# A further product in the Silu slot, statistics one piece per chunk, and gate projections in their inputs' banks: a fused attention-and-Mamba kernel

## The chip, the cores and the metric

The kernel runs on one core of one Trainium2 chip, as one launch. The metric is the device time of that core in microseconds, as the median of several executions. The engines are called PE (TensorE), DVE (VectorE), ACT (ScalarE), POOL (GpSimd) and SP (SyncE, which here issues every DMA).

## The reference, cut to what matters

`x` has 8 samples of 512 channels and 48 x 48 = 2304 tokens, in float32. Layer 0 is a linear causal attention with 8 heads on a group-normalised input, layer 1 a chain of four Mamba blocks over 128 channels each, on another group norm; each block takes the block before it as an addend.

```python
def reference(x, ...):
    x = x + _L0_conv_ref(_gn(x), Wq, bq, Wkv, bkv)      # linear causal attention
    x = x + _L1_conv_ref(_gn(x), in_proj_w, conv_w, ...)  # four Mamba blocks in a chain
    return x

def _mamba(u, Wi, wc, bc, Wx, Wdt, bdt, A_log, Dp, Wo):
    xz = u @ Wi.T
    xp, z = split(xz)                       # 256 inner channels each
    xs = silu(causal_conv4(xp, wc) + bc)
    dt, Bm, Cm = split(xs @ Wx.T)           # 8, 16 and 16 columns
    delta = softplus(dt @ Wdt.T + bdt)
    dA = exp(delta * A)                     # per channel d and state n
    dBu = (delta * xs) * Bm
    h_t = dA_t * h_{t-1} + dBu_t            # scan over 2304 tokens
    y = sum_n(h * Cm) + xs * Dp
    return (y * silu(z)) @ Wo.T

# around each block i: x_i = spx[i] + prev
fused = max(x_i, x_m)
prev = sigmoid(mean(x_i)) * x_i + sigmoid(mean(fused)) * fused
```

## The kernel before

**Jobs, slots and halves.** Tokens are cut in six chunks of 384. A *job* is one chunk of one Mamba block of one sample, 192 in all. Two streams of samples (even and odd) alternate by a fixed list of turns, since the blocks of one sample depend on each other. A job has eight *slots*; in each slot DVE does four scans (`scan`, L830) of 128 partitions x 385, each with its own pair of state and channel group. A slot has two *halves*: half 2k lies before the scans of slot k, and half 2k+1 after its second scan. At each half `beside(half)` steps other tasks that are due, so everything that isn't a scan is dealt out by half numbers. A job's halves run from 0 to 15 modulo 16; slot 7 holds 14 and 15.

**What a scan needs.** Its decays, `exp(delta * A)`, are made by ACT into a PSUM bank (`decay`, L819). Its input is a product of B and `delta * xs` in a tile `u`: the last 128 columns by POOL (`last_product`, L798), the first 256 by DVE (`product`, L809), which reads a PSUM copy `dxp` that ACT makes twice a job (`inputs`, L782). After the scans of a slot POOL multiplies u by C (`weigh`, L846) and PE gathers the sum into `yp` (`gather`, L853). There are five u buffers. In `slot(k)` the product of slot k+1 is drawn at the start of slot k, and the POOL part of slot k+2 in the middle of it.

**Banks.** Six PSUM banks serve everything but `yp` and `dxp`. `ahead(n)` makes decays in advance, up to n, while a bank is spare: DEPTH = 3 after each scan, DEPTH + 2 ahead of the table changes. `take` hands out the bank that has been spare longest, and prefers for decays those that were freed "late".

**A job's inputs.** `prepare` is a task that begins 22 halves (LEAD = 11 slots) before its job's first half, `first = 2 * self.start`, as far as its stream has declared the input `ready`. It convolves two halves of the channels on PE (`conv`, L635: eight records each), makes two gate projections (`gate`, L646), then four Silus on ACT (L670 to L675), then a projection to dt, B and C (L681, L686), then softplus (L694, L705). The Silus and softplus each need another ACT table than the exponential, so each is fenced by table loads. A stage is written `yield when, banks`; "1" means one half after the last stage, "2" two.

```python
yield "1", 1
xc0 = conv(0)
yield "2", 2
xc1 = conv(1)
zp0 = gate(0)
yield "1", 0
```

**Attention.** `chunk(m)` is one chunk of attention for 128 channels, one per job, with its stages at `times[m] + j`. `times[m]` is 3 modulo 16 in the steady part. Among its stages are the projections (L288), the features (L300, L301; L345 for q, L353 for k), the transposition of the divisor (L418) and, after the last chunk of a block, the group norm for Mamba (`group_norm`, L171 to L195), whose result lets `Stream.pass_on` make the next block's input (`xi`, L597 to L609).

**Input statistics.** `statistics(b)` loads 24 pieces of a sample (`piece`, L248) and takes `bn_stats` of each (L242), one piece every two halves, from 64 halves before the sample's attention begins. One buffer `stats_a` serves all samples.

Of the kernel before, what the change touches and what calls it, by code (L numbers as in the profile page):

```python
# [9 lines left out]
F32 = mybir.dt.float32  # L10
AF = mybir.ActivationFunctionType
# [38 lines left out]
def attention_then_mamba_kernel(  # L50
# [110 lines left out]

    def group_norm(stats, n, name, bufs):


        bank = Banks()
        yield "1", 1
        mv = small.tile([P, n, 2], F32, tag=f"mv{n}", name=f"mv_{name}", bufs=1)
# [3 lines left out]
        nc.tensor.matmul(mean_ps[:, 0:n], grp, mv[:, :, 0], start=True, stop=True)  # L171
        yield "1", 0
        gm = small.tile([P, 3, n], F32, tag=f"gm{n}", name=f"gm_{name}", bufs=1)
# [7 lines left out]
        else:  # L181
            nc.vector.tensor_mul(gm[:, 2, :], gm[:, 1, :], gm[:, 1, :])
            nc.vector.tensor_add(gm[:, 2, :], gm[:, 2, :], mv[:, :, 1])
        yield "0", 1
        var_ps = bank()
        nc.tensor.matmul(var_ps[:, 0:n], grp, gm[:, 2, :], start=True, stop=True)
        yield "1", 0
        nc.vector.tensor_scalar_add(gm[:, 2, :], var_ps[:, 0:n], 1e-5)
        bank.free()
        norm = small.tile([P, 3, n], F32, tag=f"norm{n}", name=f"norm_{name}", bufs=bufs)  # L190
        nc.gpsimd.tensor_tensor(norm[:, 0, :], gm[:, 2, :], power[:, 0:n], ALU.pow)
        yield "1", 0
        for i, factor in ((0, -1.0), (1, float(L))):
# [15 lines left out]
    def statistics(b):  # L209

        xv = x[b].rearrange("(t p) l -> p t l", p=P)
        stats = small.tile([P, 4, NC, 6], F32, tag="stats_a", name=f"stats_a{b}", bufs=1)
        if b == 0:

            xs = []

            def load(c):
                t = mpool.tile([P, 4, 1 + LC], F32, tag="u", name=f"xs_{c}", bufs=5)[:, :, 0:LC]
                nc.sync.dma_start(out=t, in_=xv[:, :, c * LC : (c + 1) * LC])
                xs.append(t)  # L220

            for c in range(5):
                load(c)
            load_projections(0)
            for c in range(NC):
                for ct in range(4):
                    nc.vector.bn_stats(stats[:, ct, c, :], xs[c][:, ct, :])
                if c == 0:
                    load(5)
                    fetch(0)  # L230
            for o in range(1, 4):
                load_projections(o)
        else:
            for ct in range(4):
                for c in range(NC):
                    yield "2", 0
                    if (ct, c) == (0, 0):
                        nxt = piece(b, 0)
                    xs = nxt
                    i = ct * NC + c + 1  # L240
                    nxt = piece(b, i) if i < 4 * NC else None
                    nc.vector.bn_stats(stats[:, ct, c, :], xs)  # L242
        norms[b] = yield from group_norm(stats, 4, f"a{b}", 2)
# [24 lines left out]
    def chunk(m):  # L268
# [99 lines left out]
        if ksum is not None:  # L368
            kept = new("kept")
            nc.scalar.copy(kept[64:128], kc[64:128])  # L370
            save(ksum[:, cols], kept[64:128])
# [84 lines left out]
        if c + 1 == NC:  # L456
            norm = yield from group_norm(stats, 1, f"m{b}_{o}", 8)
            flush()
            done[b, o] = norm
# [156 lines left out]
    class Job:  # L616
# [6 lines left out]
        def prepare(self):  # L623
# [19 lines left out]

            def gate(h):
                zp = bank()[:, 0:LC]
                nc.tensor.matmul(  # L646
# [5 lines left out]
                )  # L652
                return zp

# [3 lines left out]
            converting.append(n)  # L658
            yield "1", 1
            xc0 = conv(0)  # L660
            yield "2", 2
            xc1 = conv(1)
            zp0 = gate(0)
            yield "1", 0
            xs = self.xs = mpool.tile([P, 2, LC], F32, tag="xs", name=f"xs_{n}")
# [4 lines left out]
            nc.scalar.activation(xs[:, 0, :], xc0, AF.Silu, bias=pv[:, 0:1])  # L670
            bank.free()
            zp1 = gate(1)
            nc.scalar.activation(xs[:, 1, :], xc1, AF.Silu, bias=pv[:, 1:2])
            nc.scalar.activation(sz[0], zp0, AF.Silu)
            nc.scalar.activation(sz[1], zp1, AF.Silu)  # L675
            converting.clear()
            bank.free(3, late=True)
            yield "1", 1
# [65 lines left out]
            for h in range(2):  # L744
                yield "1", 0
                nc.gpsimd.tensor_tensor(delta[:, h, :], delta[:, h, :], xs[:, h, :], ALU.mult)  # L746
            first = 2 * self.start
            yield "2", 0
# [208 lines left out]
    def finale(job):  # L957
# [4 lines left out]
        if job.c == NC - 1:  # L962
            yield from job.stream.pass_on()

    begun, put, counted = 0, 0, list(range(1, B))

    def begin(latest):

        nonlocal begun, put
        while counted and times[parts.index((counted[0], 0, 0))] - 64 <= half_no[0]:  # L970
            tasks.append(Task(statistics(counted.pop(0))))
# [60 lines left out]
    todo = 0  # L1032
    primed = set()

# [32 lines left out]
    def slot(k):  # L1067
        job, s = at(k)
        end = k + 1 == slots or apart(k + 1)
        if not end:  # L1070
            j, r = at(k + 1)
            j.product(r, us[k + 1])
# [7 lines left out]
        for i in range(4):  # L1080
# [4 lines left out]
            if i == 1:  # L1085
# [10 lines left out]
                if not end and k + 2 < slots and not apart(k + 2):  # L1096
                    j, r = at(k + 2)
                    us[k + 2] = j.last_product(r)
                beside(2 * k + 1)
        u = us[k]  # L1100
# [91 lines left out]
```

## Time and profile before

| what | value |
|---|---|
| median of 3 runs | 9328.11 us |
| lowest and highest | 9324.06 and 9329.19 us |
| profiled execution, time | 9323.3 us |
| profiled execution, span | 9321.5 us |
| mean granted TensorE clock | 0.948 |
| instructions | 120629 |
| DMA, mean | 176 GB/s, 1642.84 MB |

In a group's row stand the line, the engine, the operation, the tiles out<-in, the shapes and the count; then the total busy time in us and the mean of one in ns; then the idle time of the engine ahead of it and what ended most of it. In a row of the timeline stand start and length in us, and in square brackets the idle time before it and its releaser. A matmul in float32 shows as two records.

| row | count | mean of one |
|---|---|---|
| scan, L830 | 6144 | 938 ns |
| decay, L819 | 6144 | 579 ns |
| product, L809 | 1536 | 1195 ns |
| POOL's part of the product, L798 | 1536 | 1276 ns |
| product with C, L846 | 1536 | 3180 ns |
| bn_stats of the input, L242 | 168 | 542 ns |
| table load ahead of the Silus, L670 | 192 | 1283 ns |
| table load ahead of softplus, L705 | 192 | 1283 ns |
| table loads ahead of decays, L819 | 382 | 1283 ns |
| gate projection records, L646 | 768 | 500 ns |

The busy times of neighbouring instructions overlap a little: scans follow each other at 0.85 us, pieces of bn_stats at 0.46.

### The profile page before, as it was taken

How to read it: one execution, taken by the hardware profiler on the slowest of the kernel's cores; microseconds unless marked ns; L12 is line 12 of the kernel's file. 1: busy time of each engine (PE TensorE's matmuls, PEld its weight loads, DVE VectorE, ACT ScalarE, POOL GpSimd, SP SyncE). 2: the span in 40 equal slices, each digit the busy share in tenths (PEclk: the TensorE clock that was granted, in tenths of full speed). 3: DMA queues.
4: the chain of work that ended last, by engine and by line, in shares of the span. 5: the costliest groups of instructions: out<-in, count | busy, mean ns of one | idle time of the engine just before them, and what ended most of it. 6: DMA issues, size and time to landing. Idle time of an engine off the chain costs nothing.

```text
span 9321.5 us, 120629 instructions
## 1 busy us (share of the span) xinstructions
PE 7735.1 (83%) x35714; PEld 3673.0 (39%) x35714; DVE 8348.4 (90%) x11640; ACT 6580.2 (71%) x12656; POOL 8080.8 (87%) x5635
## 2 busy tenths in 40 slices
PE   7888888888888888888888888888888888888865
PEld 4444444433344444443343444443333434444321
DVE  3899999999999999999999999999999999999997
ACT  3677777777777777777777777776777777777775
POOL 2788888889988898889998888888998888888998
PEclk9999999999999999999999999999999999999977
DMA  6566666667666666666766666667666666666654
GB/s 189 158 169 173 175 174 168 180 189 198 188 169 176 177 179 172 176 183 189 196 182 178 174 175 173 174 170 194 192 184 182 176 176 172 173 171 175 167 153 129
DMA packets 1002899, 1642.84 MB, mean 176 GB/s; under 512 B 138592, under 2 KB 797312, under 8 KB 1002240
## 3 DMA queue, kind: packets, MB, share of 16 engines
q1 hardware_dynamic: 1002240, 1635.13, 64.1%
q8 instruction: 283, 4.64, 0.2%
q14 instruction: 376, 3.08, 0.1%
HBM read 1309.06 MB, written 325.58 MB: 175 GB/s over the span
## 4 chain that ended last, share of the span: by engine, by line
DVE 39%; ACT 20%; PE 18%; issue 7%; DMA 7%; POOL 6%; SPq 2%; DVEq 0%; POOLq 0%; ACTq 0%
DVE u L830 23%; DVE u L809 8%; PE bank L288 7%; ACT bank L819 6%; PE bank L635 4%; POOL u L846 4%; ACT L819 3%; PE yp L853 3%; PE bank L646 2%; ACT L705 2%; DMA B<-scr 2%; DMA C<-scr 1%; ACT bank L301 1%; ACT delta L705 1%; DVE sm L436 1%
## 5 line engine op out<-in xcount | busy, mean ns | idle before, releaser
L830 DVE TENSOR_TENSOR_SCAN u<-bank,u 128x385 f32<-128x385 f32 (+1 forms) x6144 | 5475.1, 938 | 530.5 <-ACT bank L819 503.2
L846 POOL TENSOR_TENSOR u<-u,C 128x1536 f32<-128x1536 f32 x1536 | 4885.1, 3180 | 219.5 <-DVE u L830 112.6
L819 ACT ACTIVATE bank<-dr,av 128x385 f32<-128x385 f32 (+1 forms) x6144 | 3431.3, 579 | 1556.9 <-DVE u L830 1113.3
L853 PE MATMUL yp<-u,cst 128*64 128x384 f32 x12288 | 2429.9, 514 | 282.7 <-ACT yp L787 146.3
L798 POOL TENSOR_TENSOR u<-B,dxr 128x512 f32<-128x512 f32 x1536 | 1959.9, 1276 | 22.4 <-DMA dxr<-xscr 19.0
L288 PE MATMUL bank<-xn,wq_sb 128*128 128x384 f32 x4608 | 1855.1, 552 | 48.8 <-DVE u L830 31.7
L809 DVE TENSOR_TENSOR u<-B,dxp 128x1024 f32<-128x1024 f32 x1536 | 1834.7, 1195 | 10.7 <-ACT dxp L782 10.7
L853 PEld LDWEIGHTS yp<-u,cst 128*64 128x64 f32 x12288 | 788.3, 139 | 1476.6 <-issue 903.5
L635 PE MATMUL bank<-xi,wk 128*128 128x384 f32 x3072 | 1118.2, 507 | 280.1 <-ACT kl L385 172.7
L288 PEld LDWEIGHTS bank<-xn,wq_sb 128*128 128x128 f32 x4608 | 929.1, 212 | 862.9 <-issue 215.1
L635 PEld LDWEIGHTS bank<-xi,wk 128*128 128x128 f32 x3072 | 563.7, 193 | 862.2 <-ACT kl L385 254.1
L844 POOL COPY state<-u 128x4 f32<-128x4 f32 x1280 | 243.8, 190 | 740.6 <-DVE u L830 738.0
L300 ACT ACTIVATE ex<-bank,bqkv_sb 128x384 f32<-128x384 f32 x384 | 221.3, 576 | 561.6 <-PE bank L288 539.2
L787 ACT ACTIVATE yp<-xs,pv 128x384 f32<-128x384 f32 x384 | 223.4, 582 | 405.7 <-DVE yz L865 405.7
L819 ACT ACT_TABLE_LOAD x382 | 490.1, 1283 | 6.7
L746 POOL TENSOR_TENSOR delta<-delta,xs 128x384 f32<-128x384 f32 x384 | 385.8, 1005 | 95.5 <-DMA dscr<-delta 84.3
L418 PE MATMUL bank<-cst,rdb 128*128 128x128 f32 x576 | 112.7, 310 | 426.1 <-DVE u L830 334.7
L694 PE MATMUL bank<-dbc,wd 9*128 9x384 f32 x768 | 316.3, 524 | 65.1 <-ACT dbc L686 29.0
L646 PE MATMUL bank<-xi,wi 128*128 128x384 f32 x768 | 297.8, 500 | 59.8 <-ACT xs L670 59.8
L871 PE MATMUL bank<-yz,wo 128*128 128x384 f32 x768 | 297.6, 509 | 34.1 <-DVE yz L865 19.4
L449 PE MATMUL bank<-sm,v 128*64 128x128 f32 x2304 | 257.2, 301 | 42.4 <-DVE u L830 40.6
L418 PEld LDWEIGHTS bank<-cst,rdb 128*128 128x128 f32 x576 | 66.8, 153 | 558.9 <-ACT xb L601 272.5
(109 smaller groups left out, 7860.3 us busy)
## 6 DMA issues: line engine op xcount, KB each, us to landing
B<-scr SPq DMA_DIRECT2D x1536, 192.0 KB
C<-scr SPq DMA_DIRECT2D x1536, 192.0 KB
xn<-xn SPq DMA_DIRECT2D x192, 768.0 KB
dr<-dscr SPq DMA_DIRECT2D x768, 192.0 KB
dxr<-xscr SPq DMA_DIRECT2D x768, 192.0 KB
dscr<-delta SPq DMA_DIRECT2D x192, 384.0 KB
xscr<-delta SPq DMA_DIRECT2D x192, 384.0 KB
xn<-in_x SPq DMA_DIRECT2D x48, 768.0 KB
```

What stands on the lines that cost most here:

```text
L288: nc.tensor.matmul(ps, wq_sb[:, kt, j * 512 + o * P : j * 512 + (o + 1) * P], xn[:, kt, :], start=(kt == 0), stop=(kt == 3),)
L635: nc.tensor.matmul(xc, wk[:, k, h * P : (h + 1) * P], xi[:, c0 + k : c0 + k + LC], start=(k == 0), stop=(k == 3),)
L646: nc.tensor.matmul(zp, wi[:, 256 + h * P : 256 + (h + 1) * P], xi[:, c0 + 3 : c0 + 3 + LC], start=True, stop=True,)
L694: nc.tensor.matmul(vp, wd[32:41, h * P : (h + 1) * P], dbc[32:41, :], start=True, stop=True)
L746: nc.gpsimd.tensor_tensor(delta[:, h, :], delta[:, h, :], xs[:, h, :], ALU.mult)
L798: nc.gpsimd.tensor_tensor(u[:, :, :, 1 + LC - TAIL :], self.B[s % 4][:, :, cols].unsqueeze(2).to_broadcast(shape), self.dxr[s // 4][:, :, ...
L809: nc.vector.tensor_mul(u[:, :, :, 1 : 1 + LC - TAIL], self.B[s % 4][:, :, cols].unsqueeze(2).to_broadcast(shape), self.dxp.unsqueeze(1).to ...
L819: nc.scalar.activation(dA[:, cols], self.dr[h][:, g, cols], AF.Exp, scale=self.w[6][:, 2 * h + g, q + j : q + j + 1],)
L830: nc.vector.tensor_tensor_scan(u[:, j, g, cols], dA[:, cols], u[:, j, g, cols], 0.0, ALU.mult, ALU.add,)
L846: nc.gpsimd.tensor_tensor(h, h, self.C[s % 4].unsqueeze(2).to_broadcast([P, NG, 2, LC]), ALU.mult)
L853: nc.tensor.matmul(self.yp[g * 64 : g * 64 + 64, 0:LC], pair_sum, u[:, j, g, 1:], start=False, stop=(s % 4 == 3 and j == NG - 1), skip_gro ...
L871: nc.tensor.matmul(self.xm[:, 0:LC], self.w[2][:, h, :], self.yz[:, h, :], start=(h == 0), stop=(h == 1),)
```

## The change

- In slot 7 of each job (`s == 7`) the product of slot k+2 is drawn by DVE in the middle of the slot, after the second scan, and noted in `drawn`; slot k+1 then draws none at its start.
- The two gate projections write into the banks of the two convolutions, each after the Silu that reads that bank. `prepare` holds two banks at the Silus instead of up to four, and the second convolution needs one bank to be due instead of two.
- The stages of the two convolutions and of the Silus are due at `first - 21`, `first - 19` and `first - 18`, with at least 0, 2 and 1 halves since the stage before. 18 halves before a job's first half is half 14 of a job, the start of its slot 7.
- The input statistics of samples 2 to 7 take one piece per 16 halves, at half 14 for even and 15 for odd samples. A piece is loaded two halves ahead. Two `stats_a` buffers are used. Sample 1 keeps two halves per piece.
- The Mamba group norm has its stages at 28, 29, 29, 30 and 31 halves after its chunk's time instead of following at once, that is from half 15 on.
- The copy `kept` takes the tile tag `before` instead of its own.

```diff
-    def group_norm(stats, n, name, bufs):
+    def group_norm(stats, n, name, bufs, places=("1", "1", "0", "1", "1")):
         bank = Banks()
-        yield "1", 1
+        yield places[0], 1
...
-        yield "1", 0
+        yield places[1], 0
...
-        yield "0", 1
+        yield places[2], 1
...
-        yield "1", 0
+        yield places[3], 0
...
-        yield "1", 0
+        yield places[4], 0
...
-        stats = small.tile([P, 4, NC, 6], F32, tag="stats_a", name=f"stats_a{b}", bufs=1)
+        stats = small.tile([P, 4, NC, 6], F32, tag="stats_a", name=f"stats_a{b}", bufs=2)
...
-            for ct in range(4):
-                for c in range(NC):
-                    yield "2", 0
-                    if (ct, c) == (0, 0):
-                        nxt = piece(b, 0)
-                    xs = nxt
-                    i = ct * NC + c + 1
-                    nxt = piece(b, i) if i < 4 * NC else None
-                    nc.vector.bn_stats(stats[:, ct, c, :], xs)
+            when = begins[b] + b % 2
+            for i in range(4 * NC):
+                yield (when - 2, 1) if b > 1 else "1", 0
+                xs = piece(b, i)
+                yield (when, 1) if b > 1 else "1", 0
+                nc.vector.bn_stats(stats[:, i // NC, i % NC, :], xs)
+                when += PERIOD
...
-            kept = new("kept")
+            kept = new("before")
...
-            norm = yield from group_norm(stats, 1, f"m{b}_{o}", 8)
+            norm = yield from group_norm(
+                stats, 1, f"m{b}_{o}", 8, [(times[m] + j, 1) for j in (28, 29, 29, 30, 31)]
+            )
...
-            def gate(h):
-                zp = bank()[:, 0:LC]
+            def gate(h, zp):
                 nc.tensor.matmul(
                     zp,
...
-            yield "1", 1
+            first = 2 * self.start
+            yield (first - 21, 0), 1
             xc0 = conv(0)
-            yield "2", 2
+            yield (first - 19, 2), 1
             xc1 = conv(1)
-            zp0 = gate(0)
-            yield "1", 0
+            yield (first - 18, 1), 0
...
             nc.scalar.activation(xs[:, 0, :], xc0, AF.Silu, bias=pv[:, 0:1])
-            bank.free()
-            zp1 = gate(1)
+            gate(0, xc0)
             nc.scalar.activation(xs[:, 1, :], xc1, AF.Silu, bias=pv[:, 1:2])
-            nc.scalar.activation(sz[0], zp0, AF.Silu)
-            nc.scalar.activation(sz[1], zp1, AF.Silu)
+            gate(1, xc1)
+            nc.scalar.activation(sz[0], xc0, AF.Silu)
+            nc.scalar.activation(sz[1], xc1, AF.Silu)
             converting.clear()
-            bank.free(3, late=True)
+            bank.free(2, late=True)
...
+    begins = {}
+    for b in counted:
+        first = times[parts.index((b, 0, 0))]
+        begins[b] = (first - 20) // PERIOD * PERIOD - 4 * NC * PERIOD - 2 if b > 1 else first - 64
...
-        while counted and times[parts.index((counted[0], 0, 0))] - 64 <= half_no[0]:
+        while counted and begins[counted[0]] - 4 <= half_no[0]:
...
-    primed = set()
+    primed, drawn = set(), set()
...
-        if not end:
+        if not end and k + 1 not in drawn:
             j, r = at(k + 1)
             j.product(r, us[k + 1])
...
                     us[k + 2] = j.last_product(r)
+                    if s == 7:
+                        j.product(r, us[k + 2])
+                        drawn.add(k + 2)
                 beside(2 * k + 1)
```

More of the change, by code (lines that the diff above doesn't have):

```diff
@@ L652, in gate @@
                 )
-                return zp
             while converting or not st.scaled:
@@ L746, in prepare @@
                 nc.gpsimd.tensor_tensor(delta[:, h, :], delta[:, h, :], xs[:, h, :], ALU.mult)
-            first = 2 * self.start
             yield "2", 0
```

## The prediction

> **What bounds the kernel now.** I read the page's busy shares first, then the waits of VectorE (DVE), then the timeline of one job, then stretches of twelve jobs.
>
> ```profile
> PE 7735.1 (83%) x35714; PEld 3673.0 (39%) x35714; DVE 8348.4 (90%) x11640; ACT 6580.2 (71%) x12656; POOL 8080.8 (87%) x5635
> ```
>
> DVE is the fullest engine at 90%, and POOL follows at 87%. There are 1536 slots in 192 jobs, so a job takes 48.5 us of the span, and DVE idles about 5 of them. The waits say for whom (total us, times, longest):
>
> ```profile
> DVE u L830 <- ACT bank L819: 503.2, 194, 4.7
> DVE q L345 <- ACT bank L301: 141.5, 63, 6.6
> DVE gm_m L188 <- PE bank L186: 29.4, 31, 1.1
> ```
>
> The first row is the scan waiting for the exponential (the "decay") that ScalarE (ACT) makes for it. It happens 194 times, that is once a job, 2.6 us each. The timeline of one ordinary job shows where (start, length, engine, line), in three fences: DVE, ACT, PE.
>
> ```profile
> 1115.89 1.20 DVE L809 TENSOR_TENSOR u<-B,dxp 128x1024 f32<-128x1024 f32 x1
> 1117.01 2.65 DVE L830 TENSOR_TENSOR_SCAN u<-bank,u 128x385 f32<-128x385 f32 x3
> 1122.82 0.96 DVE L830 TENSOR_TENSOR_SCAN u<-bank,u 128x385 f32<-128x385 f32 x1 [3.17 <-ACT bank L819]
> 1123.69 1.19 DVE L809 TENSOR_TENSOR u<-B,dxp 128x1024 f32<-128x1024 f32 x1
> 1124.81 1.80 DVE L830 TENSOR_TENSOR_SCAN u<-bank,u 128x385 f32<-128x385 f32 x2
> ```
>
> ```profile
> 1116.39 1.11 ACT L819 ACTIVATE bank<-dr,av 128x385 f32<-128x385 f32 x2
> 1117.52 1.28 ACT L670 ACT_TABLE_LOAD   x1
> 1118.81 0.58 ACT L670 ACTIVATE xs<-bank,pv 128x384 f32<-128x384 f32 x1
> 1119.29 0.57 ACT L673 ACTIVATE xs<-bank,pv 128x384 f32<-128x384 f32 x1
> 1119.75 0.49 ACT L674 ACTIVATE sz<-bank 128x384 f32<-128x384 f32 x1
> 1120.39 0.49 ACT L675 ACTIVATE sz<-bank 128x384 f32<-128x384 f32 x1
> 1120.90 1.28 ACT L819 ACT_TABLE_LOAD   x1
> 1122.20 1.09 ACT L819 ACTIVATE bank<-dr,av 128x385 f32<-128x385 f32 x2
> ```
>
> ```profile
> 1116.18 2.85 PE L635 MATMUL bank<-xi,wk 128*128 128x384 f32 x8 [1.58 <-ACT kl L385]
> 1118.86 1.50 PE L646 MATMUL bank<-xi,wi 128*128 128x384 f32 x4
> ```
>
> From 1117.52 to 1122.20 ACT makes no decay: two table loads around four Silus. DVE has three decays in hand, does three scans of slot 7 and then stands for 3.17 us until the fourth. This is the Silu slot. One job in six misses it: after a change of block the Silus come half a slot late, and two rows of DVE show the bill, in that job and in the next:
>
> ```profile
> 1219.53 0.96 DVE L830 TENSOR_TENSOR_SCAN u<-bank,u 128x385 f32<-128x385 f32 x1 [2.36 <-ACT bank L819]
> ...
> 1235.44 0.55 DVE L345 SCALAR_TENSOR_TENSOR q<-ex,bank 128x384 f32<-128x384 f32 x1 [4.07 <-ACT bank L301]
> ```
>
> The second arises because softplus is late too, and a transpose on PE (L418) waits 3.13 us for the bank that softplus frees, with the projection for q (L288) queued behind it. Finally, twelve jobs without and with two samples' input statistics, from one Silu load to the twelfth after it:
>
> ```profile
> 1307.90:1874.60 566.70, 481.45 (x2237) 229.72 (x2236) 519.82 (x721) 406.99 (x785) 498.78 (x343) 0.96 0.65 177
> 1874.60:2454.70 580.10, 478.57 (x2225) 226.44 (x2224) 535.23 (x777) 411.20 (x793) 526.28 (x383) 0.96 0.69 192
> ```
>
> The columns are length, then busy PE, weight loads, DVE, ACT, POOL. The statistics lengthen the stretch by 13.4 us: at one piece per slot, seven of eight pieces fall outside the idle place.
>
> **The change, part by part.** I lay the ordinary job above on a clock that is 0 at 1117.01, where scan 0 of slot 7 starts.
>
> *Banks and the fourth decay.* Six banks serve all. At the Silus, three decays, two convolutions and one gate hold all six today, so ahead(5) emits nothing. With the gates written into the convolutions' own banks one is spare, and the decay for scan 3 goes out before the Silu load: 0.55 us on ACT (1.09 for two). The load moves from 0.51 to 1.06, the first Silu to 2.35.
>
> *Gates in the inputs' banks.* Each gate now waits for its own Silu. Today's second gate already does, in the late job:
>
> ```profile
> 1216.16 0.91 PE L646 MATMUL bank<-xi,wi 128*128 128x384 f32 x2 [1.36 <-ACT xs L670]
> ```
>
> There the first Silu starts at 1215.53, so a gate begins 0.63 after that and ends at 1.54. Four records take 1.50 (the L646 row of the ordinary job), so a second gate right behind ends near 2.2. The third Silu starts at 1.58 and the fourth at about 2.25; the return load starts 2.76 after the first Silu, against 2.09 today (1118.81 to 1120.90): 0.67 us more for ACT, with that load and all decays queued behind. Next decay: 2.35 + 2.76 + 1.30 (load, 1120.90 to 1122.20) = 6.41; its scan follows 0.62 later (1122.20 to 1122.82) at 7.03. On PE, the gather (L853), the 40-row projection (L681) and the rest come some 1.3 us later; PE stands 2.08 us at L418 in this job's next slot, which takes that up with little left.
>
> *The drawn product.* DVE does four scans (0.85 each, 3.41) and product k+2 (1.11) before it stands: 4.52. The new wait is 7.03 - 4.52 = 2.5 us, on scan 0 of the next slot. Today that scan starts at 1124.81, 7.80 on the clock. Gain: 0.77 us a job. Behind the product stand scans 2 and 3. It needs B rows, issued at least 8.0 and typically 13.4 us before that place, and a u buffer whose gather ended about 4 us before it; I cost both at nothing. If either were late, every microsecond shows at those scans.
>
> 128 jobs (192 less 31 late, 31 with a group norm, two at the ends, counted in the trace): -98 us.
>
> *The pinned stages.* The late job is late by one half: its input is declared ready at 22 halves before its start, just after begin() has looked. The first convolution may now go out in the half in which the job is begun (gap 0 instead of 1), and the second needs one bank instead of two, so the Silus come back to slot 7. On PE nothing stands between the preceding gather and this convolution, so it waits for xi (L609 on POOL) until the same time as now. The waits 2.36 and the average 3.3 (1.2 to 4.2, some 31 jobs) go, an ordinary 2.5 comes: -3.2 x 31 = -98. Bounds: 0 if POOL is late there, -150 with smaller waits around.
>
> *The moved group norm.* Its first step falls into half 15 (one aggregate, 0.31, hidden), the next on half 16, ahead of scan 0: it waits for a mean matmul queued behind gates, gather and L681, which I place 0.9 us after the scan could start. Idle becomes about 3.0 instead of 2.25 (rows L188 and L830): +0.75 x 31 = +23; bounds 0 and +45. Its result comes three halves later, still before the stream asks for it.
>
> *The statistics.* 144 pieces of samples 2 to 7 (bn_stats, 0.46 start to start) now lie in the Silu slot, one or two a job, hidden by the 2.5 us; three stretches like the one shown lose their 13.4: -40. If the cover were gone they would cost 66. Their 144 loads move on SP's queue to two halves ahead; the buffer is then free, so SP's 87.0 us of waiting at L248 for bn_stats goes, off the path. The second stats buffer costs no time. The ksum copy in the "before" tile adds a wait of the next "before" load on SP for the ksum store. The store is issued some six halves (18 us) earlier; I cost it at nothing, at worst a few microseconds of SP with B and C rows queued behind.
>
> Sum: -98 - 98 + 23 - 40 = -213 against this execution's own 9323.3 us, which lies 4.8 below the median of the runs shown (9328.1): 9110 and 9115. The same sum by idle time per six jobs comes out some 25 lower, since small waits (L345, L353) shrink with the late job. I take 9105.
>
> **A rule that speaks against it.** The Trainium skill, "TensorE: Matmul & The Clock Gate", section "What's actually happening": the array runs at half clock unless a recent window of about 3.4 us was busy. This kernel's trace agrees that cold windows exist: the granted clock was 0.53 in 1131.50 to 1135.00, just after PE had stood, and eight L288 records took 4.47 us instead of 2.85. The change puts two gates behind a pause, on ACT's path. By the row, a gate took 0.91 after a pause of 1.36, and the clock was 1.00 in 1118 to 1121; the new pause is about 1 us. By the rule, if that window turns cold, two gates take about 2.9 instead of 1.5: +1.4 a job over 190 jobs is +266, and the sum is +53, slower. I follow the row, since, counted by slot over the trace, slot 7 holds 2 of some 200 cold windows and slot 1 holds 110.
>
> **Rivals.**
> - *Cold gates* (slower): place L646 in slot 7, price as above, about 9380. It decides from an added 1.1 us a job (213/190), gates of 2.6 us together. For: PE does go cold after waits of 2 us. Against: the pause is half of that.
> - *Only part of it arrives*: the projection chain (L418, L288, L300) has hardly slack against q at slot 2 (24 jobs already wait 0.25 there, and k at L353 in 135), so ACT's 1.3 us may return as a wait at L345 or L353. Half of the two big terms remain: about 9215.
> - *More*: POOL keeps up, norms are free and the small waits go: -290, about 9035. Against it, POOL is busy 43.9 us of each job (526.28 / 12) in the second stretch shown, before any hand-over, so jobs cannot go far below 45 there.
> - *It doesn't do what it says*: the drawn product waits for B or u and merely moves the idle time, and the Silus of the late jobs stay late: 9320.
>
> **How the numbers follow.** Forecast 0.64 (9105, own range 9050 to 9170); partial 0.15; more 0.10; no net effect 0.04; cold gates 0.07. No change means within 0.2%, 19 us, about what a measurement of this kernel can tell. Faster by more: 0.89; same 0.04; slower 0.07. The range 9015 to 9215 reaches to the middle of the partial case and past the better one.
>
> **What would show it.** Right: L830 waiting for L819 about 2.5 us on scan 0 of slot 0 in every job, two products in slot 7, four decays before the Silu load, the return load 2.8 us after the first Silu; no L345 waits of 4 us; bn_stats only in slot 7; L188's wait replaced by one at the mean (L174). Wrong: L646 records far over 0.5 us, a product L809 with a wait of its own in slot 7, new waits at L345 or L353, or POOL's wait for L830 (738.0 us) nearly gone.

## The result, and the profile after

The changed kernel takes 9251.11 us (median of four runs, 9239.89 to 9258.27) against 9327.1 for the kernel before (four runs): a ratio of 0.9918, 95% interval 0.9901 to 0.9935. It is faster by 76 us, where the prediction of 9105 meant 222, and it lies above the range, whose upper end was 9215. The profiled execution took 9239.89 us, its span is 9238.1 against 9321.5, its mean granted clock 0.967 against 0.948.

The page's first row after, and the longest waits of DVE (total us, times, longest). Scans are now L828, q L343, k L351, ACT's Exp for both L299, the projection L286, the gather L851.

```profile
PE 7626.0 (83%) x35714; PEld 3583.9 (39%) x35714; DVE 8342.1 (90%) x11640; ACT 6616.7 (72%) x12656; POOL 8081.8 (87%) x5635
```

```profile
DVE u L828 <- issue: 297.2, 205, 3.9
DVE k L351 <- ACT bank L299: 152.3, 137, 3.6
DVE gm_m L174 <- PE bank L171: 73.5, 32, 2.9
DVE norm_m L195 <- POOL norm_m L191: 38.7, 32, 1.4
DVE q L343 <- ACT bank L299: 30.5, 15, 5.8
```

DVE does the same work as before (8342.1 us of it, 8348.4 before), so the whole gain is idle time of DVE: span less busy time went from 973.1 to 896.0, by 77. Adding up the waits of each line over all releasers shows where it went:

| DVE waits, us | before | after | difference |
|---|---|---|---|
| scans (L830, now L828) | 530.3 | 396.1 | -134.2 |
| group norm reading PE (L174 and L188) | 31.8 | 75.3 | +43.5 |
| q (L345 and L423, now L343) | 145.3 | 30.5 | -114.8 |
| these three | 707.4 | 501.9 | -205.5 |
| k (L353, now L351) | 70.8 | 152.3 | +81.5 |
| group norm's last stage, waiting for POOL (L195) | 0.7 | 38.7 | +38.0 |
| statistics waiting for a load (L242, now L239) | 15.4 | 25.5 | +10.1 |

The rows on which the prediction was built gave 205.5 us of the predicted 213. Two rows that it held at nothing, k and the norm's last stage, took 120 back. That 205.5 lies so near 213 is in part chance: the single terms, below, came out further off.

The Silu slot came out as drawn up. DVE, ACT and PE in one ordinary job (start, length, engine, line):

```profile
1060.09 1.79 DVE L828 TENSOR_TENSOR_SCAN u<-bank,u 128x385 f32<-128x385 f32 x2
1061.80 1.19 DVE L807 TENSOR_TENSOR u<-B,dxp 128x1024 f32<-128x1024 f32 x1
1062.91 0.55 DVE L239 BATCH_NORM_STATS2 stats_a<-xs 128x6 f32<-128x384 f32 x1
1063.38 1.79 DVE L828 TENSOR_TENSOR_SCAN u<-bank,u 128x385 f32<-128x385 f32 x2
1066.77 1.81 DVE L828 TENSOR_TENSOR_SCAN u<-bank,u 128x385 f32<-128x385 f32 x2 [1.60 <-issue]
```

```profile
1059.15 1.59 ACT L817 ACTIVATE bank<-dr,av 128x385 f32<-128x385 f32 x3
1060.77 1.28 ACT L668 ACT_TABLE_LOAD   x1
1062.06 0.58 ACT L668 ACTIVATE xs<-bank,pv 128x384 f32<-128x384 f32 x1
...
1063.65 0.49 ACT L673 ACTIVATE sz<-bank 128x384 f32<-128x384 f32 x1 [0.53 <-PE bank L645]
1064.29 0.49 ACT L674 ACTIVATE sz<-bank 128x384 f32<-128x384 f32 x1 [0.15 <-PE bank L645]
1064.80 1.28 ACT L817 ACT_TABLE_LOAD   x1
1066.09 0.59 ACT L817 ACTIVATE bank<-dr,av 128x385 f32<-128x385 f32 x1
```

```profile
1062.70 1.56 PE L645 MATMUL bank<-xi,wi 128*128 128x384 f32 x4 [1.05 <-ACT xs L668]
```

The Silu load starts 0.68 after the first scan of slot 7 (predicted 1.06), the return load 2.74 after the first Silu (predicted 2.76). Four scans and the product run before DVE stands, and the scan it stands at is scan 0 of the next slot. The row blames "issue", but the ACT fence shows its decay ending at 1066.68, 0.09 ahead of it. The two gates, four records, took 1.56 us; no half-clock stretch lies there.

So ordinary jobs should be 0.77 us shorter. Some are: outside the statistics' stretches most took 46.2 to 46.6 us before, and most come in two kinds now, of 45.5 to 45.8 and of 47.2 to 47.5. PE in slots 1 and 2 tells them apart. First a short job, then a long one, with the k of the long one on DVE:

```profile
980.16 0.52 PE L416 MATMUL bank<-cst,rdb 128*128 128x128 f32 x3 [0.85 <-DVE u L828]
980.91 2.85 PE L286 MATMUL bank<-xn,wq_sb 128*128 128x384 f32 x8 [0.23 <-DVE u L828]
...
987.00 1.51 PE L851 MATMUL yp<-u,cst 128*64 128x384 f32 x8 [1.90 <-ACT yp L785]
988.44 2.85 PE L286 MATMUL bank<-xn,wq_sb 128*128 128x384 f32 x8
```

```profile
1032.79 2.20 PE L851 MATMUL yp<-u,cst 128*64 128x384 f32 x8 [2.00 <-ACT yp L785]
1034.92 3.81 PE L286 MATMUL bank<-xn,wq_sb 128*128 128x384 f32 x8
```

```profile
1039.82 0.55 DVE L351 SCALAR_TENSOR_TENSOR k<-ex,bank 128x384 f32<-128x384 f32 x1 [1.89 <-ACT bank L299]
```

In both PE stands some 2 us ahead of the gather L851, which waits for ACT to add the skip into yp. In the long one the projection for k behind it takes 3.81 us instead of 2.85, the gather 2.20 instead of 1.51. The granted clock changes only on a fixed grid of 3.413 us. These are the windows of that grid at the two pauses, two for the short job and two for the long one (length, then busy PE, weight loads, DVE, ACT, POOL, granted clock, DMA share, GB/s):

```profile
982.27:985.69 3.42, 2.83 (x9) 1.25 (x7) 3.06 (x5) 3.39 (x6) 3.34 (x4) 1.00 1.06 246
985.69:989.10 3.41, 2.10 (x10) 1.06 (x11) 3.41 (x7) 3.41 (x8) 3.41 (x3) 1.00 0.48 177
1030.06:1033.47 3.41, 1.42 (x8) 0.53 (x9) 3.28 (x7) 3.41 (x9) 3.41 (x2) 1.00 0.70 235
1033.47:1036.89 3.42, 3.42 (x9) 1.44 (x6) 3.42 (x4) 1.82 (x5) 3.42 (x5) 0.50 0.16 61
```

The short job's pause is split by the grid: PE is busy 2.83 and 2.10 us of the two windows, and the clock stays full. The long job's pause falls whole into one window, with PE busy 1.42 us, and the next window is granted half. Before, the pause lay elsewhere. PE of the kernel before:

```profile
1131.08 0.52 PE L418 MATMUL bank<-cst,rdb 128*128 128x128 f32 x3 [2.08 <-DVE u L830]
1131.84 4.47 PE L288 MATMUL bank<-xn,wq_sb 128*128 128x384 f32 x8 [0.24 <-DVE u L830]
...
1138.14 1.51 PE L853 MATMUL yp<-u,cst 128*64 128x384 f32 x8 [0.54 <-ACT yp L787]
```

There the half clock fell on the projection for q, which nobody was yet waiting for, and the gather came after a pause of 0.54. Now PE comes later to L416, the pause there is 0.85, q is projected at full clock, and the pause of 2 us stands before the gather, where the half clock falls on k, for which DVE waits. Over the whole kernel the pauses of PE before L416 fell from 426 to 165 us and those before the gather rose from 282 to 436. In 58 jobs DVE now waits over 1 us for k, 115 us in all; before, in 14. In 57 of the 58 a half-clock stretch begins 11 to 17 us after the job's first scan, and only two other jobs have one there. Jobs with such a stretch take 47.5 us in the median, the others 45.8.

### The profile page after: what moved, and what is told of

Same layout as the page of the kernel before. It is cut to its first block, busy times and chain, and to the rows that moved or that the text cites. A ratio compares the mean times of both kernels' runs of the same rounds, so it can differ in the third digit from the quotient of the medians.

```text
span 9238.1 us, 120657 instructions
## 1 busy us (share of the span) xinstructions
PE 7626.0 (83%) x35714; PEld 3583.9 (39%) x35714; DVE 8342.1 (90%) x11640; ACT 6616.7 (72%) x12656; POOL 8081.8 (87%) x5635
## 4 chain that ended last, share of the span: by engine, by line
DVE 30%; ACT 24%; POOL 15%; PE 11%; issue 9%; DMA 8%; SPq 2%; POOLq 0%; DVEq 0%; ACTq 0%
DVE u L828 19%; POOL u L844 9%; ACT bank L817 9%; DVE u L807 6%; PE bank L286 5%; POOL u L796 4%; PE yp L851 3%; ACT L817 3%; ACT L668 2%; PE bank L645 2%; ACT L704 2%; DMA wk<-in_wconv 1%; SPq L737 1%; ACT bank L299 1%; DMA before<-ksum 1%
## 5 line engine op out<-in xcount | busy, mean ns | idle before, releaser
L828 DVE TENSOR_TENSOR_SCAN u<-bank,u 128x385 f32<-128x385 f32 (+1 forms) x6144 | 5467.4, 939 | 396.3 <-issue 297.2
L851 PE MATMUL yp<-u,cst 128*64 128x384 f32 x12288 | 2422.9, 515 | 437.4 <-ACT yp L785 279.7
L286 PE MATMUL bank<-xn,wq_sb 128*128 128x384 f32 x4608 | 1699.6, 513 | 83.1 <-DVE u L828 41.8
L851 PEld LDWEIGHTS yp<-u,cst 128*64 128x64 f32 x12288 | 779.1, 139 | 1622.0 <-issue 1130.6
L286 PEld LDWEIGHTS bank<-xn,wq_sb 128*128 128x128 f32 x4608 | 861.0, 197 | 866.9 <-DVE u L828 165.5
L680 PE MATMUL bank<-xs,wx 128*40 128x384 f32 x768 | 279.8, 487 | 0.0
L645 PEld LDWEIGHTS bank<-xi,wi 128*128 128x128 f32 x768 | 130.4, 190 | 374.8 <-ACT xs L668 316.1
```

Source lines behind the costliest of these rows:

```text
L286: nc.tensor.matmul(ps, wq_sb[:, kt, j * 512 + o * P : j * 512 + (o + 1) * P], xn[:, kt, :], start=(kt == 0), stop=(kt == 3),)
L645: nc.tensor.matmul(zp, wi[:, 256 + h * P : 256 + (h + 1) * P], xi[:, c0 + 3 : c0 + 3 + LC], start=True, stop=True,)
L828: nc.vector.tensor_tensor_scan(u[:, j, g, cols], dA[:, cols], u[:, j, g, cols], 0.0, ALU.mult, ALU.add,)
L851: nc.tensor.matmul(self.yp[g * 64 : g * 64 + 64, 0:LC], pair_sum, u[:, j, g, 1:], start=False, stop=(s % 4 == 3 and j == NG - 1), skip_gro ...
```

## The experiments

Theory A: k is late by the half clock after PE's pause. Rival B: k is late because PE and ACT reach it later, whatever the clock. On the parts of the change: theory C, with shared banks the drawn product adds nothing, since DVE would do the next product ahead of the waiting scan anyway; theory D, the shared banks lose against banks of their own for the gates. The ratios are to the kernel before, measured on the same chip, with 95% intervals. The runs come from several chips, on which the kernel before took 9317.78 to 9329.24 us, so differences between runs are read from the ratios, and one of 0.001 is worth 9.3 us.

| run | median us | ratio |
|---|---|---|
| w_after | 9260.68 | 0.993 (0.9918 to 0.9943) |
| w_before | 9578.25 | 1.0268 (1.0254 to 1.0282) |
| w2_after | 9168.47 | 0.9841 (0.9827 to 0.9856) |
| k_early | 9151.65 | 0.9809 (0.9796 to 0.9823) |
| k_before | 9316.99 | 0.9986 (0.9978 to 0.9995) |
| u_drawn | 9241.44 | 0.9907 (0.9893 to 0.9921) |
| u_gates | 9141.42 | 0.9816 (0.9801 to 0.9831) |
| k_gates | 9062.06 | 0.9716 (0.9702 to 0.9731) |
| k_gates_nodraw | 9286.95 | 0.9968 (0.9956 to 0.9979) |
| k_norm | 9150.6 | 0.9811 (0.9795 to 0.9827) |
| k_pins | 9220.76 | 0.9888 (0.9873 to 0.9903) |
| k_stats | 9216.61 | 0.9893 (0.9876 to 0.9909) |
| best | 9023.89 | 0.9673 (0.9657 to 0.9689) |

### Keeping PE busy in the pause: w_after, w_before

Seven matmuls more behind the output projection in slot 2, into columns of yp that nobody reads; in the one kernel and in the other.

```diff
-    nc.tensor.matmul(yp[:, 0:LC], ident, cst[:, 0:LC], start=True, stop=True)
+    nc.tensor.matmul(yp, ident, cst[:, 0:512], start=True, stop=True)
...
         job.project()
+        for _ in range(7):
+            nc.tensor.matmul(
+                yp[:, LC:512], ident, mask, start=False, stop=True, skip_group_check=True
+            )
```

> The changed kernel with seven extra matmuls of 128 x 128 on PE in every job, right behind the output projection in slot 2, into columns of the yp bank that nothing reads; nothing else differs. Theory A (clock): in 59 jobs of the changed kernel the 2 us pause of PE ahead of the gather in slot 2 makes the granted clock fall just when k is projected, and DVE waits some 1.9 us for k (L351). Filling the pause keeps the clock up: the waits of DVE for k fall from 152 us to about 50, the time from 9251 to about 9150 (59 x 1.7 us less). Theory B (k is late because the Silu stage became 1.3 us longer on ACT and PE): more work on PE changes nothing or makes k later, 9250 to 9300.

> The kernel before with the same seven extra matmuls at the same place. Theory A: its clock falls in slot 1, where the projection of q is covered, so the extra matmuls help nothing: 9327 within 15 us, its waits for k (L353) stay near 71 us. Theory B says the same. A gain of 50 us or more would say that the pause in slot 2 cost the kernel before as well, and that the extra matmuls are no test of the change.

A miss. The mean clock rose from 0.967 to 0.981 and the waits of 1.9 us at k are gone, yet nothing was gained: DVE now waits for k in nearly every job, 0.8 us on average. The waits of w_after on DVE, then its PE:

```profile
DVE k L351 <- ACT bank L299: 146.6, 186, 5.2
```

```profile
1048.79 1.72 PE L959 MATMUL yp<-cst 128*128 128x128 f32 x14
...
1051.28 1.51 PE L851 MATMUL yp<-u,cst 128*64 128x384 f32 x8 [0.77 <-ACT yp L785]
```

Though the columns are others, ACT's write to yp stood until the extra matmuls were through, and the gather after it. In the kernel before the same matmuls cost 250 us. Two rows of DVE's waits grew: scans waiting for decays, which ACT makes after that write (503.2 before), and k (70.8 before):

```profile
DVE u L830 <- ACT bank L819: 624.0, 343, 4.7
DVE k L353 <- ACT bank L301: 184.6, 186, 2.2
```

The probe carried a wait of its own, so the pair decides nothing between A and B.

### The same without touching yp: w2_after

```diff
         job.project()
+        for _ in range(5):
+            nc.tensor.matmul(
+                job.xm[:, LC:512], ident, mask, start=False, stop=True, skip_group_check=True
+            )
```

> The changed kernel with five extra matmuls of 128 x 128 behind the output projection in slot 2, now into unread columns of that projection's own bank, since in the first such kernel ACT's write to the yp bank waited for the extra matmuls in every job. Theory A (clock): no cold window at the projection of k, L351 waits near 50 us, and no new wait: 9251 - 100, about 9150. Theory B (k is late by the longer Silu stage): the waits for k stay, 9250.

The five matmuls go into the bank that the output projection itself has just written. The clock rises to 0.981 again. Stretches at half clock fall from 128 to 63, and those that begin 11 to 17 us after a job's first scan from 59 to 3. DVE's wait:

```profile
DVE k L351 <- ACT bank L299: 58.6, 141, 3.6
```

PE does more work than in the changed kernel, and the kernel is faster by 0.0077 of the time before, 72 us. A holds and B falls: the work in front of k is the same or more, and only the clock is better. The 58.6 us at k that are left, in waits of 0.4 us on average, are no more than the 70.8 of the kernel before, so B has nothing to claim.

### DVE asks for q and k half a slot later: k_early, k_before

```diff
         ex = feature(qp, qb)
+        yield at(1, 0), 1
+        kp, kb = project(1)
         yield at(2), 0
         q = new("q", 2)
         nc.vector.scalar_tensor_tensor(q, ex, 1.0, qp, ALU.min, ALU.add)
         bank.free()
-        yield at(2, 0), 1
-        kp, kb = project(1)
```

> The changed kernel with k projected one half earlier, behind the feature of q and ahead of the gather in slot 2, which holds one more bank for that half. Theory A: the projection fills PE's pause and no longer stands behind it; waits for k fall to about 20 us, the time to about 9140. Theory B says the same for k. If the additional bank costs decays in slot 2, new waits of the scan appear there, up to 0.9 us a job (170 us), and the time stays near 9250.

> The kernel before with k projected one half earlier, nothing else: what the change is worth when k never waits on either side. Theory A (the clock window at k hides the change's gain): the kernel before waits only 71 us for k, so it gains at most that, 9260 to 9330, and against the changed kernel with the same edit (9152) the change is worth 110 to 175 us instead of 76. Rival (k early is simply a better order, whatever the change): it gains the same 100 us here, about 9227.

The edit was meant to bring the projection for k one half earlier, into PE's pause. It did not: PE still takes it behind the gather, and still stands there. PE of k_early, then its DVE in the same job:

```profile
1037.08 2.83 PE L851 MATMUL yp<-u,cst 128*64 128x384 f32 x8 [1.99 <-POOL u L844]
1039.83 3.18 PE L286 MATMUL bank<-xn,wq_sb 128*128 128x384 f32 x8
```

```profile
1039.95 0.54 DVE L345 SCALAR_TENSOR_TENSOR q<-ex,bank 128x384 f32<-128x384 f32 x1
...
1045.88 0.54 DVE L351 SCALAR_TENSOR_TENSOR k<-ex,bank 128x384 f32<-128x384 f32 x1
```

The likely reason is that no bank was spare in the earlier half; the later steps slid instead: DVE takes q at the start of slot 3 and k at the start of slot 4, half a slot later than in the changed kernel. The half clock is still there (51 half-clock stretches at that place), and nobody waits for it: k's waits fall from 152.3 to 11.3 us, those at L450, which adds attention's result to x, rise from 30.6 to 88.0, and the kernel gains 100. The expected mechanism was wrong; that the number fitted was luck. It still serves as a state in which k is off the path. In the kernel before, the same edit gives only 10 us, since waits at the output gate, and at L452 (from 26.3 to 83.8), take the place of those at q and k:

```profile
DVE fg L882 <- PE bank L871: 110.8, 53, 4.1
```

With k off the path on both sides, the change is worth 0.9986 - 0.9809 = 0.0177, or 165 us, where it gave 76 as it stands.

### Is it the drawn product, or the banks: u_drawn, u_gates, k_gates, k_gates_nodraw

u_drawn and k_gates_nodraw leave the product of slot k+2 where it was, the one in the changed kernel, the other in k_gates:

```diff
-                    if s == 7:
+                    if s == 8:
```

u_gates and k_gates give the gates banks of their own again, and keep the drawn product, the one in the changed kernel, the other in k_early:

```diff
-            yield (first - 19, 2), 1
+            yield (first - 19, 2), 2
             xc1 = conv(1)
+            zp0 = bank()[:, 0:LC]
+            gate(0, zp0)
...
-            gate(0, xc0)
+            bank.free()
+            zp1 = bank()[:, 0:LC]
+            gate(1, zp1)
             nc.scalar.activation(xs[:, 1, :], xc1, AF.Silu, bias=pv[:, 1:2])
-            gate(1, xc1)
-            nc.scalar.activation(sz[0], xc0, AF.Silu)
-            nc.scalar.activation(sz[1], xc1, AF.Silu)
+            nc.scalar.activation(sz[0], zp0, AF.Silu)
+            nc.scalar.activation(sz[1], zp1, AF.Silu)
             converting.clear()
-            bank.free(2, late=True)
+            bank.free(3, late=True)
```

> The changed kernel without the drawn product: the product of slot 1 is drawn at the start of slot 0 as before, everything else as changed. Theory C: the stall now stands on scan 0 of slot 0, and at the start of slot 0 the product lies ahead of that scan in DVE's queue anyway, so drawing it earlier gains nothing; what gains is the fourth decay that the spare bank allows: 9251 within 15 us. Rival (the product pays): 1.1 us a job over 190 jobs come back, about 9450.

> The changed kernel, k as changed, with the gate projections in banks of their own again. Theory D: 0.4 to 0.5 us a job less at the Silus as in the kernel with k early, so 9251 - 90, about 9160; the cold windows at k may come more or less often, 50 us either way. The prediction's own term (the shared banks pay 0.77 us a job): about 9370.

> The changed kernel with k projected early, and the gate projections back in banks of their own (the second convolution is due with two banks again); the drawn product stays. Theory D (the shared banks and the drawn product pay for the same stall, and either would do): with three decays and the product drawn, the scan that waits is scan 3 of slot 7, 5.8 us after scan 0, and scan 0 of slot 0 starts at 6.7 instead of 7.0: 0.35 us a job less, 9152 - 60, about 9095. The prediction's own term (the fourth decay pays 0.77 us a job): 9152 + 120, about 9275.

> The kernel with k projected early and the gates in their own banks, now without the drawn product. Theory D: the product then lies behind the waiting scan 3 again, 1.1 us a job for the 160 jobs that stand there: 9062 + 180, about 9240. If the product pays nothing here either, 9062.

Without the drawn product the changed kernel stands at 0.9907 instead of 0.9918, no difference that can be told. With own banks it stands at 0.9816 (k_gates against k_early: 0.9716 against 0.9809), so beside the drawn product the shared banks lose 87 to 95 us. With own banks the drawn product is worth 0.9968 - 0.9716 = 0.0252, or 235 us. C and D both hold. The banks are not without use: k_early, which has them and the product, stands 0.0159 or 148 us below k_gates_nodraw, which has neither. Both fill the same wait, and the product alone fills it better than the pair. DVE's idle time at the Silus shows it, added up from the first scan of slot 7 to the second of the next slot 0, mean of a hand-over (us), jobs without and with the group norm's mean there; before, the 31 late jobs count among those without:

| kernel | without the norm | with the norm |
|---|---|---|
| before | 2.85 | 2.23 |
| after | 2.15 | 2.47 |
| u_drawn | 2.16 | 2.48 |
| u_gates | 1.73 | 1.44 |
| k_gates | 1.69 | 1.44 |
| k_gates_nodraw | 2.81 | 2.61 |

Two waits of k_gates on DVE, then the same place of a job as shown above, and its ACT:

```profile
DVE u L830 <- ACT bank L819: 329.2, 208, 4.4
...
DVE gm_m L174 <- PE bank L171: 0.5, 1, 0.5
```

```profile
1093.82 1.20 DVE L809 TENSOR_TENSOR u<-B,dxp 128x1024 f32<-128x1024 f32 x1
1094.93 0.56 DVE L239 BATCH_NORM_STATS2 stats_a<-xs 128x6 f32<-128x384 f32 x1
1095.40 0.94 DVE L830 TENSOR_TENSOR_SCAN u<-bank,u 128x385 f32<-128x385 f32 x1
1097.46 2.66 DVE L830 TENSOR_TENSOR_SCAN u<-bank,u 128x385 f32<-128x385 f32 x3 [1.12 <-ACT bank L819]
```

```profile
1093.45 0.58 ACT L670 ACTIVATE xs<-bank,pv 128x384 f32<-128x384 f32 x1
...
1095.55 1.28 ACT L819 ACT_TABLE_LOAD   x1
```

Only three decays are in hand there (the inputs hold three of the six banks at the Silus, not up to four), so DVE stands at scan 3 of slot 7, with the next product behind that scan: drawing a product ahead of it fills the wait. With shared banks scan 3 has its decay, DVE stands at scan 0 of the next slot, and the product of that slot stands ahead of it by itself; the gates behind their Silus cost ACT 0.64 us (2.74 against 2.10 from Silu to return load). The wait of 73.5 at L174 goes too: the gates no longer stand ahead of the norm's mean on PE.

### The other parts put back in k_early: k_norm, k_pins, k_stats

```diff
@@ k_norm @@
-            norm = yield from group_norm(
-                stats, 1, f"m{b}_{o}", 8, [(times[m] + j, 1) for j in (28, 29, 29, 30, 31)]
-            )
+            norm = yield from group_norm(stats, 1, f"m{b}_{o}", 8)
@@ k_pins @@
-            yield (first - 21, 0), 1
+            yield "1", 1
             xc0 = conv(0)
-            yield (first - 19, 2), 1
+            yield "2", 1
             xc1 = conv(1)
-            yield (first - 18, 1), 0
+            yield "1", 0
@@ k_stats @@
-                yield (when - 2, 1) if b > 1 else "1", 0
+                yield "1", 0
                 xs = piece(b, i)
-                yield (when, 1) if b > 1 else "1", 0
+                yield "1", 0
...
-        begins[b] = (first - 20) // PERIOD * PERIOD - 4 * NC * PERIOD - 2 if b > 1 else first - 64
+        begins[b] = (first - 20) // PERIOD * PERIOD - 4 * NC * PERIOD - 2 if b > 8 else first - 64
```

> The changed kernel with k projected early, and the group norm of Mamba following at once as before. The prediction's term: 23 us better, 9130; by the changed kernel's waits (L174 74 us and L195 39 us against 29 us at L188 before) up to 84 us better, 9070. Rival: at its old place the norm holds a bank at the Silus in 31 jobs, which takes the fourth decay or delays a convolution by half a slot there: 0.9 to 3 us each, so 9152 to 9220.

> The changed kernel with k projected early, and the stages of convolutions and Silus following each other by gaps as before instead of at fixed halves. The prediction's term: the Silus of 31 jobs come half a slot late again, 3.2 us each: 9152 + 98, about 9250. Rival (since the second convolution needs only one bank now, the Silus are on time without the fixed halves): 9152 within 15 us.

> The changed kernel with k projected early, and the input statistics of samples 2 to 7 at one piece every two halves again. The prediction's term: 40 us more, 9192; if all 126 pieces that leave the Silu slot show (0.46 us each), 9210. Rival (the stretches with statistics are bound by POOL): 9152 within 15 us.

Against k_early's 0.9809: the old norm places change nothing (0.9811), the old gaps of the stages cost 0.0079 or 74 us, the old pace of the statistics 0.0084 or 78 us. In k_pins the late jobs are back: in 29 jobs the Silu load begins some 2.4 us after the first scan of slot 7, where nearly all of k_early's begin within 1 us, and a wait at the output gate has come:

```profile
DVE fg L880 <- PE bank L869: 113.0, 38, 5.1
```

k_stats is not quite the old order: it loads a piece one half before its use, where the kernel before loaded it one piece, two halves, ahead. Some 23 of its 78 us are waits for such loads, at samples 2 to 7:

```profile
DVE stats_a L239 <- DMA xs<-in_x: 50.0, 30, 3.7
```

These do not add up. With pins, statistics and norm as in the change, but neither shared banks nor drawn product, k_gates_nodraw stands at 0.9968, 0.0018 from k_before. So pins, paced statistics and the moved norm together bring next to nothing where the Silu slot has no room, and what taking one out costs is not what it alone brings.

### The best version

The norm's last stage waits for POOL's power (L191) in every block. k_gates with that stage two halves later:

```diff
-                stats, 1, f"m{b}_{o}", 8, [(times[m] + j, 1) for j in (28, 29, 29, 30, 31)]
+                stats, 1, f"m{b}_{o}", 8, [(times[m] + j, 1) for j in (28, 29, 29, 30, 33)]
```

> The changed kernel with k projected early, the gates in banks of their own, and the last stage of Mamba's group norm two halves later (33 instead of 31). If the wait of DVE for POOL's power (L195, 1.2 us in 31 jobs) is part of what the moved norm costs, it goes: 9062 - 35, about 9027, or in ratio to the kernel before 0.968 instead of 0.972. If the later norm holds up the stream's next input instead, 9062 or more.

9023.89 us, 0.0043 or 40 us less than k_gates and 303 less than the kernel before on that chip (9326.66). In k_gates DVE waited at L195; here that row is gone:

```profile
DVE norm_m L195 <- POOL norm_m L191: 43.6, 31, 2.2
```

## Why the prediction was wrong

- *What bounds it*: right. DVE's work stayed, and what it idled less is the gain.
- *Banks, the fourth decay, the gates' own price*: right in each step, load, gates, return load and order of scans. The wait fell by 2.85 - 2.15 = 0.70 us in the table, and by 0.83 (2.93 to 2.10) if the late jobs of the kernel before are left out, where 0.77 was predicted.
- *The drawn product*: the time is right and the credit wrong. The four scans and one product ahead of the wait were counted correctly, but that product stands there undrawn as well: u_drawn. Banks and product were taken as two means to one gain; they are two ways to fill the same wait, and by u_gates and k_gates the product with own banks gains more.
- *The pinned stages*: q's waits went from 145 to 31 us, as said. By k_pins, with k off the path, the term is 74 us against 98.
- *The moved group norm*: the wait at L174 appeared, 2.3 us a block, where about 3.0 was given. The step that failed is "Its result comes three halves later, still before the stream asks for it": the norm's own last stage on DVE asks first, and POOL's power is late for it by 1.2 us in each of 32 blocks, 38 us. That POOL queue was not weighed. `best`, which puts the stage off, gains 40. With the old places (k_norm), though, the kernel is no slower and no faster than k_early: the waits at L174 and L195 fall by 101 us, and in their place those of the scans rise by 63 and those at L399 by 18, while DVE is busy 25 us longer.
- *The statistics*: predicted 40. The two stretches read for it hold 13 and 35 pieces, not none and all 48; the twelve jobs ahead of them, which hold none, took the same 566.70 us as the first, so 13.4 was still near. Twelve jobs around each change of samples (the 33rd to 44th from the start, and so on every 48) took 9.0 us per six jobs more than the next twelve, and now 4.8, which makes 25 us over the 36 jobs. The waits for late loads at L239 that came in addition, 10 us, lie in the first 100 us, at sample 1, whose pieces are now loaded one half ahead. Taken out of k_early the paced statistics cost 78, 23 of them by such loads; there the Silu slot has the room that it lacked before.
- *The term that is missing*, and the one that decides: PE's 1.3 us. The step that failed is the one by which PE's stand of 2.08 us at L418 "takes that up with little left". That stand was no slack to be used up: PE did the work later, and stood as long further on, ahead of the gather (2.08 and 0.54 us at the two places before, 0.85 and 1.90 now), and the half clock that follows such a stand went with it from q, where it was free, to k, where it is not. The prediction had this cost in its trace (4.47 us instead of 2.85 for eight L288 records), and asked only whether it would fall on the gates. w2_after gives its price as 72 us; k_early, which also takes away k's short waits, gives 100.
- *Rivals*: "Only part of it arrives" named the place (k at L353) and gave 9215; 9251 is worse than it. Its reason was ACT's 1.3 us, which B stands for; the clock is what did it. Cold gates did not come.

With the two rows of the table, 82 and 38, put into the sum as costs, -213 becomes -93; of the 17 to the measured -76, the loads at L239 are 10. This closes the account of DVE's idle time, not that of each term, since the terms don't add up. Why the jobs around the change of samples keep 4.8 us per six is open. DVE is busy there with 3.6 us more of pieces and some 5 us more of the input's own group norm (L169 to L195) than in the next twelve jobs, but no run took these away.

## What to carry to other kernels

Work put into an engine's idle time doesn't use that time up when the engine was waiting for another: it pushes the wait to the next place, and with it whatever follows a wait (here a half clock), so follow it to the next thing that someone needs. A saving that rests on two edits should be tried with each alone: here the product alone was worth 235 us and the pair 148. And parts that fill the same wait are not to be added.

## What the runs showed of the hardware

- In these traces PE drops to half clock for the next window of 3.4 us when it was too little busy in the last. In the traces of before and after, the changes of the granted clock (411 and 255, the end of the trace left out) lie within 1 ns of a grid of 3.413 us. On this grid, a window at full clock with PE busy under 40% was followed by a half-clock one every time (138 of 138 before, 70 of 70 after), one with 40 to 50% in about half of them (30 of 54, 45 of 90), one with more in 38 of 2241 and 13 of 2355. A stand of 2 us can be enough, if it falls whole into one window as at 1030.06, and is not if the grid splits it as at 982.27: hence jobs of 45.8 and of 47.5 us from the same instructions. The Trainium skill, "TensorE: Matmul & The Clock Gate", section "HAM oscillation — how this bites in real kernels", gives as the abstract rule "no PE-idle gaps >~3.4µs"; by these counts that is too mild for this kernel.
- Matmuls into columns of a PSUM tile that nobody reads made ACT's write to its other columns wait for them (w_after, w_before). Whether the chip or the dependencies that the program states are the reason was not tried.
